# Conditioned two-stage block on one core: loads of the first half reordered, first rows stored through the scalar queue, weight sums, scales and token sums placed elsewhere

## The chip, the core and the metric

One core of a Trainium2 chip runs the whole block. The metric is device time in microseconds (us), the median of the timed runs. Engine names are those of the profile: PE multiplies matrices (PEld is its weight load), DVE is the vector engine, ACT the scalar engine, POOL the general-purpose engine, SP the engine that mostly issues DMAs. A name with a q (SPq, ACTq) is the issue of a DMA by that engine's queue. The profile's numbers come from one profiled execution.

## The reference, cut to what is computed

There are 32 sequences of 128 tokens with 512 features, one condition vector for each sequence, and a mask of tokens.

```python
emb = silu(t) @ ada_w + ada_b                      # [32, 1536]
shift, scale, gate_msa = split(emb, 3, axis=1)
norm = where(m, layernorm(x) * (1 + scale) + shift, 0)
fwd = gelu(norm @ ssm_w1 + ssm_b1, exact) @ ssm_w2 + ssm_b2
bwd = flip(gelu(flip(norm) @ bwd_w1 + bwd_b1, exact) @ bwd_w2 + bwd_b2)
x = x + gate_msa * where(m, fwd + bwd, 0)
shift_mlp, scale_mlp, gate_mlp = split(silu(t) @ ffada_w + ffada_b, 3, axis=1)
h = gelu((layernorm(x) * (1 + scale_mlp) + shift_mlp) @ ff_w1 + ff_b1, tanh)
out = x + gate_mlp * (h @ ff_w2 + ff_b2)
```

The two branches of the first half act on each token alone, so the kernel treats them as one network with 1024 hidden features, and it runs this first half only for the masked tokens. The second half runs for all 4096 tokens, in float32.

## The kernel before, in words

**First half.** The masked tokens are gathered into 512 slots: four chunks of 128 slots, two chunks (256 slots, "s0") first and two ("s1") later. The kernel first loads ada_w in `load_ada` (L124): four loads of columns 0 to 1023 (L128, shift and scale), then one load of columns 1024 to 1535 (L130, the gate). From these `modulation` makes rows of mod1 in PE (`pm_ss` for shift and scale, `pm_g` for the gate). `slot_part` (L274) spreads such rows over the slots, `modulated` (L167, L168, DVE) normalises, `transposed_slots` (L175, PE, and a copy by ACT, L176) turns the chunk, and `hidden` (L184 in PE, L188 in ACT) makes the eight parts of the hidden layer, each of four multiplications and one activation. `project` (L198) multiplies back, one multiplication for each of the eight parts, and DVE adds the bias (L200), multiplies by the gate (L201) and adds the row itself (L289). `finish_slots` stores the 128 rows into x1_rows in DRAM (L290). There are four such stores.

**Order.** From the opening on, each engine carries out its instructions in the order of the program (a manual schedule), so the order of the lines is the order of every queue. DMAs of SP and ACT share eight completion semaphores in turn: an issue waits for the DMA that used its semaphore eight issues earlier. A DMA is thus never only a transfer, it is also a place in SP's or ACT's program.

**What stands where before.** `pm_g` is multiplied in four blocks of k, strewn between the turning of the two chunks (L495 to L524); its tile of ada_w shares a buffer with the next one, ffada_w, whose load (L128 again, `ada_f`) thus waits for the last block. After the first six parts of s0 and the projections of s0 come pm_f (the second half's modulation, L254), eight parts of s1 (`ph_s`, L184) and the projections of s1, `po_s` 2 and 3.

**Second half.** The 32 sequences go in four pairs of groups of four. Both products use a scheme of seven block products (named P1 to P7) with sums of blocks: sums of weight blocks made once (`Weights.combine`, L308; `weight_sums`, L577, whose four results go through DRAM as t_rows and come back as `tw`), and sums of token blocks (`TokenBlocks.one`, L757; `token_sums`, L817 to L827). Pair 0 is prepared during the end of the first half: `take_first_half` (L656, POOL) gathers x1_rows over the rows of x for the masked tokens and so waits for the stores of L290; `Statistics` (L688, L689) and `normalised` (L700) work on DVE; side 0 is turned by DVE (L1132) and sixteen DMAs (`turned`, L727, eight by SP and eight by ACT); side 1 is turned by PE (`transposed`, L716). `scale_and_shift` then applies scale and shift of the sequence, by DVE (L708) or ACT (L710). Then `FirstProduct` begins (L888 in PE).

These are the lines around the junction:

```python
    h1 = hidden(xT_t, NH, w1, 0, AF.Gelu, "s1", ssm)
    nc.scalar.activation(warm, biasT[0:1, 0:1], AF.Gelu_apprx_tanh)
    ...
    turned(xn, xT[0], (nc.sync, nc.scalar))
    for k in range(KC // 2, KC):
        scaled(0, xT[0], k)
    ...
    finish_slots(2, h1, gs[0])
```

Of the kernel before, what the change touches and what calls it, by code (L numbers as in the profile page):

```python
# [9 lines left out]
F32 = mybir.dt.float32  # L10
# [3 lines left out]
AF = mybir.ActivationFunctionType  # L14
# [8 lines left out]
def kernel(  # L23
# [49 lines left out]
    nc = tc.nc  # L73
# [40 lines left out]
    def broadcast_rows(t, vec, queue):  # L114

        n = vec.shape[0] // D
        each = t.shape[0] // n
        for j in range(n):
            queue.dma_start(
                t[j * each : (j + 1) * each, :],  # L120
                vec[ts(j, D)].rearrange("(o d) -> o d", o=1).to_broadcast([each, D]),
            )

    def load_ada(w, which, split):  # L124

        t = adap.tile([P, KC, 3 * D], F32, tag="ada", name=f"ada_{which}")
        for k in range(KC):
            nc.sync.dma_start(t[:, k, :split], w[ts(k, P), :split])  # L128
        if split < 3 * D:
            nc.sync.dma_start(  # L130
                t[:, :, split:], w[:, split:].rearrange("(k p) d -> p k d", p=P)
            )
        return t

    modb_a = adap.tile([3 * B, D], F32, tag="modb", name="modb_a", bufs=1)
# [5 lines left out]
    w2 = ssm.tile([P, HC, D], F32, name="w2")  # L141
    ada_a = load_ada(ada_w, "a", 2 * D)


# [46 lines left out]

    def project(i, h, w, bias, gate, name, between=None):

        po = ps_o.tile([P, 512], F32, tag="o", name=f"po_{name}_{i}")
        for f in range(HC):
            if between and f in between:
                between[f]()
            nc.tensor.matmul(po, h[f][:, ts(i, P)], w[:, f, :], start=(f == 0), stop=(f == HC - 1))  # L198
        t = tp.tile([P, D], F32, tag="t", name=f"t_{name}_{i}")
        nc.vector.tensor_tensor(t, po, bias, ALU.add)  # L200
        nc.vector.tensor_tensor(t, t, gate, ALU.mult)  # L201
        return t
# [48 lines left out]
    def modulation_matmuls(pm, ada, lo, hi, blocks):  # L251
        for k in blocks:
            for j in range(lo, hi):
                nc.tensor.matmul(  # L254
                    pm[ts(j, B), :],
                    sT[:, k, :],
                    ada[:, k, ts(j, D)],
                    start=(k == 0),
                    stop=(k == KC - 1),
                )  # L260

    def modulation_rows(pm, mod, modb, lo, hi):
        rows = slice(lo * B, hi * B)
        nc.vector.tensor_tensor(mod[rows], pm[rows], modb[rows], ALU.add)
# [14 lines left out]
    def slot_part(at, j, pool, tag):  # L279
        return of_slots(pick, at, mod1, j, pool, tag, f"part{j}_s{at}")  # L280
# [6 lines left out]
    def finish_slots(at, h1, gate, between=None):  # L287
        t = project(at % (NC // 2), h1, w2, b2, gate, f"s{at}", between)
        nc.vector.tensor_tensor(t, t, xc[at], ALU.add)  # L289
        nc.sync.dma_start(x1_rows[ts(at, P), :], t)  # L290

# [31 lines left out]
    def load_x(p, spare=()):  # L323
        return [load_side(p, side, spare[2 * side : 2 * side + 2]) for side in range(2)]
# [136 lines left out]

    for j, w in enumerate((ssm_w1, bwd_w1)):
        part = w1[:, :, ts(j, D)]
        nc.gpsimd.memset(part[0:1, 0, 0:1], 0.0)
        nc.sync.dma_start(part, w.rearrange("(k p) f -> p k f", p=P))
    for j, w in enumerate((ssm_w2, bwd_w2)):
        part = w2[:, ts(j, KC), :]
        nc.gpsimd.memset(part[0:1, 0, 0:1], 0.0)
        nc.sync.dma_start(part, w.rearrange("(k p) f -> p k f", p=P))
    for key, vec in (("ssm1", ssm_b1), ("bwd1", bwd_b1), ("ff1", ff_b1)):  # L470
# [15 lines left out]
    rows = [(slot_part(c, 1, ps_o, "o"), slot_part(c, 0, ps_h, "h")) for c in range(2)]  # L486
    pm = ps_o.tile([P, 512], F32, tag="o", name="pm_g")
    xT_s = ssm.tile([P, KC, NH], F32, tag="xT", name="xT_s0", bufs=2)
# [8 lines left out]
    ]  # L497
    modulation_matmuls(pm, ada_a, 2, 3, range(2))
    fw1 = fwp.tile([P, KC, FF], F32, name="fw1")
# [9 lines left out]
    for t, vec in ((b2, ssm_b2), (b2b, bwd_b2), (modb_f, ffada_b), (fb2, ff_b2)):  # L509
        broadcast_rows(t, vec, nc.sync)  # L510
    nc.sync.dma_start(fw2, ff_w2.rearrange("(k p) f -> p k f", p=P))
    x_of = {0: load_x(0)}
    transposed_slots(xn_s[0], xT_s[:, :, ts(0, P)], "s0")
    modulation_matmuls(pm, ada_a, 2, 3, range(2, 3))
    token_i = find_slots(1)
    gather_slots(token_i)
    transposed_slots(xn_s[1], xT_s[:, :, ts(1, P)], "s1")
    modulation_matmuls(pm, ada_a, 2, 3, range(3, KC))
    ptr = ps_t.tile([P, 512], F32, tag="tr", name="ptr_b")
# [4 lines left out]
    nc.vector.tensor_copy(slot_i, ptr[:, n_bias : n_bias + B])  # L524
    modulation_rows(pm, mod1, modb_a, 2, 3)

# [31 lines left out]
    }  # L558
    t_sum[3], t_sum[4] = t_sum[1], t_sum[2]

# [27 lines left out]
    for c in range(2):  # L588
        h1 += hidden(xT_s, NH, w1, 0, AF.Gelu, "s0", ssm, range(4 * c, 4 * c + 3))
        rows = slot_part(2 + c, 1, ps_o, "o"), slot_part(2 + c, 0, ps_o, "o")  # L590
        gs.append(keep_gate(c, slot_part(c, 2, ps_o, "o")))
        xn_s.append(modulated(xc[2 + c], *rows, f"s{2 + c}", xn[:, 2 + c]))
        if c == 0:
            Weights(fw1, KC // 2, FF // 2, t_1).combine(0, 1, 2, 3)
        h1 += hidden(xT_s, NH, w1, 0, AF.Gelu, "s0", ssm, range(4 * c + 3, 4 * c + 4))
        if c == 1:
            transposed_slots(xn_s[0], xT_t[:, :, ts(0, P)], "s2")
# [5 lines left out]
    finish_slots(0, h1, gs[0])  # L603
    transposed_slots(xn_s[1], xT_t[:, :, ts(1, P)], "s3")
    nc.vector.tensor_scalar(modb_f[B : 2 * B], modb_f[B : 2 * B], 1.0, None, ALU.add)
    finish_slots(1, h1, gs[1])
# [40 lines left out]
    nc.vector.tensor_tensor(fb2_step, fb2[:, D // 2 :], fb2[:, : D // 2], ALU.subtract)  # L647
    weight_sums(3)
    weight_sums(4)
# [61 lines left out]

    def transposed(g, xn, xT, k, by_vector):

        ptr = ps_t.tile([P, 512], F32, tag="tr", name=f"ptr_{g}_{k}")
        for i in range(G):
            nc.tensor.transpose(ptr[:, ts(i, P)], xn[i][:, ts(k, P)], ident)  # L716
        for i in range(G):
            scale_and_shift(xT[:, k, ts(i, P)], ptr[:, ts(i, P)], k, g * G + i, by_vector)

# [8 lines left out]

    def scaled(g, xT, k, by_vector=False):

        for i in range(G):
            t = xT[:, k, ts(i, P)]
            scale_and_shift(t, t, k, g * G + i, by_vector)

# [380 lines left out]
    nc.gpsimd.dma_start(gate_rows, mod2[2 * B : 3 * B, :])  # L1115
    h1 = hidden(xT_t, NH, w1, 0, AF.Gelu, "s1", ssm)
    nc.scalar.activation(warm, biasT[0:1, 0:1], AF.Gelu_apprx_tanh)
    fw2_of = Weights(fw2, HC // 2, D // 2, t_2)
# [11 lines left out]
    for i in range(G):  # L1130
        t = stats[0].normalised(i, xn[:, :, i])
        nc.vector.transpose(t, t)  # L1132
    turned(xn, xT[0], (nc.sync, nc.scalar))
    for k in range(KC // 2, KC):
        scaled(0, xT[0], k)
# [4 lines left out]
    for c in range(2):  # L1140
        both = ssm.tile([P, 2, D], F32, tag="xT", name=f"xn_0_1_{c}", bufs=2)
        for i in range(2):
            xn_b.append(stats[1].normalised(2 * c + i, both[:, i]))
    finish_slots(2, h1, gs[0])

    def turn(k):
        transposed(1, xn_b, xT[1], k, by_vector=k < KC // 2)

    def turn_and_scale(k):
        turn(k)  # L1150
        scaled(0, xT[0], k, by_vector=True)

    finish_slots(
        3,
        h1,
        gs[1],
        {3: lambda: turn_and_scale(0), 5: lambda: turn_and_scale(1), 7: lambda: turn(2)},
    )
    turn(3)
    of_x[0] = TokenBlocks(0, xT)  # L1160
    for j in (1, 2, 3):
        of_x[0].one(j)
# [10 lines left out]
    now.do(1, "P2", "P5", "P6")  # L1173
    of_x[0].one(4)
    now.do(2, "P5")
    now.do(1, "P7")
    now.with_p5(2, "22")
    now.seed(2)
    now.do(1, "P3")
    now.with_p5(2, "12")  # L1180
    for n in range(4):
        now.token_sums(1, n)
    now.do(2, "P2", "P6")
# [5 lines left out]
    for p in range(NP):  # L1189
# [4 lines left out]
        def put(w, n, f, *args):  # L1194
            fills.setdefault(w, {}).setdefault(n, []).append(lambda: f(*args))
# [19 lines left out]
        if more_pairs:  # L1215
            if p == 0:
                x_of[1] = load_x(1, spare)
                put(4, 1, fw2_of.combine, 0)
                put(5, 1, fw2_of.combine, 1)
            x_next = x_of[p + 1]  # L1220
# [110 lines left out]
    with tc.If(more > 0):  # L1331
# [11 lines left out]
        with tc.For_i(0, more, 1):  # L1343
# [12 lines left out]
            for half_no, (mod, was, wbs, bias, bcol, func) in enumerate(  # L1356
# [20 lines left out]
                gate_l = of_slots(pick_l, 0, mod, 2, ps_h, "h", f"gate_l{half_no}")  # L1377
                t = project(0, h_l, wb, bias, gate_l, f"l{half_no}")
                nc.vector.tensor_tensor(xl, xl, t, ALU.add)
# [58 lines left out]
```

## Time and profile before

| what | value |
|---|---|
| median of 3 runs | 471.65 us (471.02 to 471.98) |
| the profiled execution's own time | 470.92 us |
| its span, first to last instruction | 469.2 us |
| PE busy | 452.4 us, 96% |
| DVE busy | 334.0 us, 71% |
| ACT, POOL busy | 174.9 us, 159.4 us |
| mean granted PE clock | 0.995 |
| DMA | 70.41 MB, mean 150 GB/s |

The page has a table of the span in 40 slices of 11.73 us. Beside it the trace answers by stretches of time (busy time of each engine, the granted clock, the DMA engines' share), by waits (who waited for whom, in total, how often, the longest), and by instructions in order of time: start, duration, engine, line, operation, tiles, number of such instructions, and in brackets the idle time before with what ended it. Rows that merge several instructions give the time from the first to the last end.

### The profile page before, as it was taken

The numbers are of one execution on the slowest core, as the hardware profiler recorded it, in microseconds if no ns is written. First come the engines' busy times: TensorE is split into PE (matmuls) and PEld (weight loads), VectorE is DVE, ScalarE is ACT, GpSimd is POOL, SyncE is SP. The second block draws the span as 40 slices with busy tenths as digits, with TensorE's granted clock in tenths as the row PEclk, the third lists the DMA queues.
The fourth block names the chain that finished last, engine by engine and source line by source line (L and its number), as shares of the span: only waits on it lengthen the run. The fifth ranks groups of instructions, "written<-read, shape, count | busy, mean of one in ns | idle before, by whom it ended". The sixth has DMA issues, their size and how long they took to land.

```text
span 469.2 us, 5826 instructions
## 1 busy us (share of the span) xinstructions
PE 452.4 (96%) x2000; PEld 365.3 (78%) x2000; DVE 334.0 (71%) x538; ACT 174.9 (37%) x380; POOL 159.4 (34%) x151
## 2 busy tenths in 40 slices
PE   6899999897999999999999999999999999999995
PEld 2475384475878888888888888888888888888884
DVE  4649377999778966997687498967873995434645
ACT  3131022543365074153643712545537134462000
POOL 6200063046876000189740003897100024660000
PEclk9999999999999999999999999999999999999999
DMA  8999943490413861854068528240863341213012
GB/s 278 386 408 362 394 172 53 86 345 19 121 44 134 137 90 49 312 174 163 1 194 106 106 98 288 102 161 3 217 100 88 125 168 62 96 64 117 0 76 107
DMA packets 82194, 70.41 MB, mean 150 GB/s; under 512 B 63136, under 2 KB 63664, under 8 KB 81138
## 3 DMA queue, kind: packets, MB, share of 16 engines
q1 hardware_dynamic: 67298, 57.95, 40.1%
q0 software_dynamic: 4256, 10.75, 6.8%
q10 hardware_dynamic: 10608, 1.32, 2.0%
q8 instruction: 17, 0.28, 0.2%
q14 instruction: 15, 0.12, 0.1%
HBM read 56.83 MB, written 13.17 MB: 149 GB/s over the span
## 4 chain that ended last, share of the span: by engine, by line
PE 61%; POOL 6%; ACT 6%; DVE 5%; issue 2%; POOLq 0%; DVEq 0%
PE a_o L1068 18%; PE e_o L1068 16%; PE a_m L888 14%; PE e_m L888 12%; ACT hb L850 2%; POOL hb L972 2%; ACT ha L850 1%; POOL ha L972 1%; POOL ha L939 1%; POOL rstd L694 1%; DVE xT L827 1%; PE last L1068 1%; DVE sx L817 1%; ACT a_o L1014 1%; ACT e_o L1014 1%
## 5 line engine op out<-in xcount | busy, mean ns | idle before, releaser
L939 POOL TENSOR_TENSOR ha<-p_m,ha 128x512 f32<-128x512 f32 x20 | 27.2, 1361 | 152.7 <-ACT ha L946 143.4
L1068 PE MATMUL e_o<-fw,ha 128*128 128x256 f32 x256 | 57.9, 379 | 0.0
L710 ACT ACTIVATE xT<-xT,modT 128x128 f32<-128x128 f32 x104 | 41.0, 480 | 40.2 <-DMA xT<-xn 39.7
L1068 PE MATMUL a_o<-t,hb 128*128 128x256 f32 x240 | 54.1, 379 | 0.0
L1068 PEld LDWEIGHTS e_o<-fw,ha 128*128 128x128 f32 x256 | 48.6, 190 | 6.6
L1068 PEld LDWEIGHTS a_o<-t,hb 128*128 128x128 f32 x240 | 45.6, 190 | 6.2
L656 POOL DMA_INDIRECT x<-x_rows,slot_i x32 | 36.6, 1144 | 30.2 <-DMA x_rows<-t_s 21.3
L850 ACT ACTIVATE hb<-hb,biasT 128x256 f32<-128x256 f32 x64 | 29.0, 500 | 29.9 <-POOL hb L972 19.3
L939 POOL TENSOR_TENSOR hb<-p_m,hb 128x512 f32<-128x512 f32 x20 | 29.8, 1489 | 18.2 <-DVE hb L918 17.9
L902 ACT COPY p_m<-e_m 128x512 f32<-128x512 f32 x27 | 15.8, 585 | 50.4 <-PE e_m L888 47.1
L946 ACT COPY ha<-e_m 128x512 f32<-128x512 f32 x32 | 18.5, 577 | 30.6 <-PE e_m L888 28.6
L1068 PE MATMUL e_o<-fw,s 128*128 128x256 f32 x128 | 29.2, 381 | 0.5 <-DVE s L1022 0.4
L1068 PE MATMUL a_o<-fw,ha 128*128 128x256 f32 x128 | 29.0, 380 | 0.0
L1068 PE MATMUL a_o<-t,s 128*128 128x256 f32 x128 | 28.9, 379 | 0.0
L184 PE MATMUL ph_s<-xT_s,w 128*128 128x256 f32 x128 | 28.7, 382 | 0.0
L198 PE MATMUL po_s<-w,h_s 128*128 128x512 f32 x64 | 28.5, 592 | 0.0
L1068 PEld LDWEIGHTS e_o<-fw,s 128*128 128x128 f32 x128 | 24.1, 190 | 4.9 <-DVE s L1022 1.7
L184 PEld LDWEIGHTS ph_s<-xT_s,w 128*128 128x128 f32 x128 | 24.0, 190 | 4.7 <-ACT h_s L188 1.5
L1068 PEld LDWEIGHTS a_o<-fw,ha 128*128 128x128 f32 x128 | 24.2, 190 | 3.5 <-ACT a_o L1014 0.2
L1068 PEld LDWEIGHTS a_o<-t,s 128*128 128x128 f32 x128 | 24.3, 190 | 3.3
L913 DVE TENSOR_TENSOR e_m<-a_m,ha 128x512 f32<-128x512 f32 x20 | 13.9, 696 | 17.1 <-POOL ha L939 6.6
L850 ACT ACTIVATE ha<-e_m,biasT 128x256 f32<-128x256 f32 x48 | 20.0, 467 | 14.9 <-PE e_m L888 9.6
(206 smaller groups left out, 878.1 us busy)
## 6 DMA issues: line engine op xcount, KB each, us to landing
tw<-t_rows SPq DMA_DIRECT2D x16, 896.0 KB, 5.2
x<-in_x_dram SPq DMA_DIRECT2D x16, 512.0 KB, 9.3
gate<-gate_rows POOLq DMA_DIRECT2D x8, 1024.0 KB
out_dram<-x SPq DMA_DIRECT2D x15, 512.0 KB, 3.1
xT<-xn SPq DMA_DIRECT2D x92, 64.0 KB, 2.7
fw<-in_L_cond_ff_w_dram SPq DMA_DIRECT2D x2, 2048.0 KB
ada_f<-in_L_cond_ffada_w_dram SPq DMA_DIRECT2D x4, 768.0 KB, 13.6
ada_a<-in_L_cond_ada_w_dram SPq DMA_DIRECT2D x4, 512.0 KB, 5.5
```

The lines of the kernel that those rows point to most:

```text
L184: nc.tensor.matmul(ph[:, :n], w[:, k, ts(f, P)], xT[:, k, :], start=(k == 0), stop=(k == KC - 1))
L198: nc.tensor.matmul(po, h[f][:, ts(i, P)], w[:, f, :], start=(f == 0), stop=(f == HC - 1))
L656: nc.gpsimd.indirect_dma_start(out=xs[i // G][i % G // 2][:, i % 2], out_offset=None, in_=x1_rows[:slots, :], in_offset=bass.IndirectOffse ...
L710: nc.scalar.activation(out, src, AF.Identity, bias=shift, scale=scale)
L850: nc.scalar.activation(dst[:, n], src[:, n], AF.Gelu_apprx_tanh, bias=biasT[:, f : f + 1])
L888: nc.tensor.matmul(bank[:, ts(n, QT)], self.w_block(j, product)[:, ts(n, P)], self.x_block(j, product), start=(product in ("P1", "P5") and ...
L902: nc.scalar.copy(p5, e)
L913: nc.vector.tensor_tensor(e, a, p5, add)
L939: nc.gpsimd.tensor_tensor(self.place(RESULT[j], c), self.p5[j], other, ALU.add)
L946: nc.scalar.copy(self.place(RESULT[j], c), src)
L972: nc.gpsimd.tensor_tensor(part, self.place("21", c), part, ALU.add)
L1068: nc.tensor.matmul(part, src[:, k, ts(i, P)], w[product][:, k, :], start=(last and k == 0), stop=True, skip_group_check=True,)
```

## The change

The order of loads on SP becomes: columns 0 to 1023 of ada_w, ssm_w1, (behind the first gathers) bwd_w1, ada_w's gate columns, ssm_w2, bwd_w2, ff_w1, ffada_w, biases, the rows of x, and only then ff_w2. `pm_g` is multiplied in one piece after the first three hidden parts of s0. The first two stores of x1_rows go by ACT's queue instead of SP's. `weight_sums(3)` moves up, between the two projections of s0, and gets a tile of its own; `weight_sums(4)` stays, into the tile of the first sums. Of the hidden layer of s1, the turning DMAs of ACT are issued between the seventh and the eighth part. ACT scales all of side 0, DVE all of side 1. The projection of chunk 3 is split: its multiplications, then the first token block sum, then its DVE part. The fourth token block sum follows the others, the token sums of stream 1 are spread over the first product, and two weight sums of ff_w2 each move one window earlier.

```diff
-        if split < 3 * D:
-            nc.sync.dma_start(
-                t[:, :, split:], w[:, split:].rearrange("(k p) d -> p k d", p=P)
-            )
         return t
+
+    def load_blocks(t, w, behind_gathers=True):
+        if behind_gathers:
+            nc.gpsimd.memset(t[0:1, 0, 0:1], 0.0)
+        nc.sync.dma_start(t, w.rearrange("(k p) f -> p k f", p=P))
...
     ada_a = load_ada(ada_w, "a", 2 * D)
+    load_blocks(w1[:, :, :D], ssm_w1, behind_gathers=False)
...
     def finish_slots(at, h1, gate, between=None):
-        t = project(at % (NC // 2), h1, w2, b2, gate, f"s{at}", between)
+        keep_slots(at, project(at % (NC // 2), h1, w2, f"s{at}", between), gate)
+
+    def keep_slots(at, po, gate):
+        t = gated(po, b2, gate, f"s_{at}")
         nc.vector.tensor_tensor(t, t, xc[at], ALU.add)
-        nc.sync.dma_start(x1_rows[ts(at, P), :], t)
+        queue = nc.scalar if at < NC // 2 else nc.sync
+        queue.dma_start(x1_rows[ts(at, P), :], t)
...
-    for j, w in enumerate((ssm_w1, bwd_w1)):
-        part = w1[:, :, ts(j, D)]
-        nc.gpsimd.memset(part[0:1, 0, 0:1], 0.0)
-        nc.sync.dma_start(part, w.rearrange("(k p) f -> p k f", p=P))
-    for j, w in enumerate((ssm_w2, bwd_w2)):
-        part = w2[:, ts(j, KC), :]
-        nc.gpsimd.memset(part[0:1, 0, 0:1], 0.0)
-        nc.sync.dma_start(part, w.rearrange("(k p) f -> p k f", p=P))
+    load_blocks(w1[:, :, D:], bwd_w1)
+    load_blocks(ada_a[:, :, 2 * D :], ada_w[:, 2 * D :])
+    load_blocks(w2[:, :KC], ssm_w2)
+    load_blocks(w2[:, KC:], bwd_w2)
...
-    modulation_matmuls(pm, ada_a, 2, 3, range(2))
...
+    x_of = {0: load_x(0)}
     nc.sync.dma_start(fw2, ff_w2.rearrange("(k p) f -> p k f", p=P))
-    x_of = {0: load_x(0)}
     transposed_slots(xn_s[0], xT_s[:, :, ts(0, P)], "s0")
-    modulation_matmuls(pm, ada_a, 2, 3, range(2, 3))
...
-    modulation_matmuls(pm, ada_a, 2, 3, range(3, KC))
...
-    modulation_rows(pm, mod1, modb_a, 2, 3)
...
         h1 += hidden(xT_s, NH, w1, 0, AF.Gelu, "s0", ssm, range(4 * c, 4 * c + 3))
+        if c == 0:
+            pm = ps_o.tile([P, 512], F32, tag="o", name="pm_g")
+            modulation(pm, mod1, ada_a, modb_a, 2, 3)
...
     transposed_slots(xn_s[1], xT_t[:, :, ts(1, P)], "s3")
+    t_sum[3] = [in_blocks(group_of_tiles("tw_3"))]
+    weight_sums(3)
...
-    weight_sums(3)
     weight_sums(4)
...
-    h1 = hidden(xT_t, NH, w1, 0, AF.Gelu, "s1", ssm)
-    nc.scalar.activation(warm, biasT[0:1, 0:1], AF.Gelu_apprx_tanh)
...
+    h1 = hidden(xT_t, NH, w1, 0, AF.Gelu, "s1", ssm, range(HC - 1))
     turned(xn, xT[0], (nc.sync, nc.scalar))
-    for k in range(KC // 2, KC):
+    h1 += hidden(xT_t, NH, w1, 0, AF.Gelu, "s1", ssm, range(HC - 1, HC))
+    nc.scalar.activation(warm, biasT[0:1, 0:1], AF.Gelu_apprx_tanh)
+    for k in range(KC):
         scaled(0, xT[0], k)
...
-    finish_slots(
-        3,
-        h1,
-        gs[1],
-        {3: lambda: turn_and_scale(0), 5: lambda: turn_and_scale(1), 7: lambda: turn(2)},
-    )
-    turn(3)
+    po = project(1, h1, w2, "s3", {1: turn(0), 3: turn(1), 5: turn(2), 7: turn(3)})
     of_x[0] = TokenBlocks(0, xT)
-    for j in (1, 2, 3):
+    of_x[0].one(1)
+    keep_slots(3, po, gs[1])
+    for j in (2, 3, 4):
         of_x[0].one(j)
...
-    of_x[0].one(4)
+    now.token_sums(1, 0)
     now.do(2, "P5")
     now.do(1, "P7")
     now.with_p5(2, "22")
     now.seed(2)
+    now.token_sums(1, 1)
     now.do(1, "P3")
     now.with_p5(2, "12")
-    for n in range(4):
-        now.token_sums(1, n)
+    now.token_sums(1, 2)
+    now.token_sums(1, 3)
...
-                put(4, 1, fw2_of.combine, 0)
-                put(5, 1, fw2_of.combine, 1)
+                put(3, 1, fw2_of.combine, 0)
+                put(4, 1, fw2_of.combine, 1)
```

## The prediction, made before the changed kernel had run

> **What bounds the kernel now.** I read the page first. PE is the bound, and the last 350 us give nearly nothing back; what this change touches lies in the first 140 us, slices 0 to 11.
>
> ```profile
> span 469.2 us, 5826 instructions
> PE 452.4 (96%) x2000; PEld 365.3 (78%) x2000; DVE 334.0 (71%) x538; ACT 174.9 (37%) x380; POOL 159.4 (34%) x151
> PE   6899999897999999999999999999999999999995
> DMA  8999943490413861854068528240863341213012
> ```
>
> The DMA engines are full in slices 1 to 4 (11.7 to 58.6 us), PE is full from slice 2 on with two dents. So I asked next who made PE wait, over the whole span (total us, times, longest):
>
> ```profile
> PE e_m L888 <- DVE e_m L932: 2.7, 2, 2.4
> PE e_m L888 <- ACT e_m L934: 1.3, 1, 1.3
> PE a_m L888 <- DVE hb L918: 1.1, 2, 0.8
> PE part_s L274 <- DVE mod L264: 0.8, 1, 0.8
> PE ptr_s L175 <- DVE xn_s L168: 0.6, 1, 0.6
> ```
>
> All but the last two lie between 90 and 133 us, where the first product begins: DVE is the late one there. The beginning, in order of time on PE:
>
> ```profile
> 14.74 1.90 PE L254 MATMUL pm_g<-ada_a,sT 128*32 128x512 f32 x4
> 17.19 0.65 PE L175 MATMUL ptr_s<-ident,xn_s 128*128 128x128 f32 x4 [0.55 <-DVE xn_s L168]
> 17.78 1.04 PE L254 MATMUL pm_g<-ada_a,sT 128*32 128x512 f32 x2
> 18.75 0.71 PE L216 MATMUL pl_s<-rank,pick 32*128 32x128 f32 x4
> 19.39 0.66 PE L175 MATMUL ptr_s<-ident,xn_s 128*128 128x128 f32 x4
> 19.98 1.04 PE L254 MATMUL pm_g<-ada_a,sT 128*32 128x512 f32 x2
> 21.18 1.13 PE L184 MATMUL ph_s<-xT_s,w 128*128 128x256 f32 x4
> ```
>
> The pm_g rows fill time in which PE waits for DVE's xn_s; from 21.18 on PE runs without a gap to 82 us. Last, the junction to the second half, from the views in order of time:
>
> ```profile
> 60.80 1.34 POOL L656 DMA_INDIRECT x<-x_rows,slot_i  x1 [21.34 <-DMA x_rows<-t_s]
> 72.53 0.47 ACT L188 ACTIVATE h_s<-ph_s,biasT 128x256 f32<-128x256 f32 x1 [1.25 <-PE ph_s L184]
> 77.16 6.66 ACTq L727 DMA_DIRECT2D xT<-xn  x8
> 86.94 3.19 ACT L710 ACTIVATE xT<-xT,modT 128x128 f32<-128x128 f32 x8 [12.42 <-DMA xT<-xn]
> ```
>
> The eighth activation of s1 (72.53) comes before ACT's eight DMA issues, which take 6.66 us. The change puts it behind them.
>
> **The change part by part**, against the profiled execution (470.92 us; span 469.2). The median is 0.73 us higher, and I add that at the end.
>
> *A. pm_g in one piece: +3.0.* Its four blocks go from idle or nearly idle places into the gapless stretch. A block is 1.90 - 1.04 = 0.86 us, four are 3.4. Against this, the turn of the second chunk waits only for its xn_s (DVE's L168 for it ends at 18.65) instead of running from 19.39, ACT's copy of it (0.58) ends near 19.97 instead of 20.66, and the first ph_s can start at about 20.05 instead of 21.18: -1.1. The weights for it now come right behind the first ada_w loads, 1 MB in the place of 1 MB, so the gathers behind them see the same queue. The gate's slot part now needs mod from pm_g: DVE's 0.69 (L264) hides behind the other two slot parts, but these three ran side by side (26.56 until ph_s at 27.63) and now the gate runs after the pair: one more 0.86 less the overlap, +0.7. Sum -1.1 + 3.4 + 0.7 = +3.0. Bounds: +4.1 if the bias rows or weights keep ph_s at 21.18, +2.3 if the three slot parts still overlap.
>
> *Loads: 0.* ada_f now waits for the later pm_g (28.8 instead of 21.05), but SP's wait rows show ff_w1, ahead of it in the same queue, landing only at 32; the cover is 3 us, and without it everything behind would slip by what is missing. The rows of x land before ff_w2 instead of behind it, about 5 us earlier; nothing waits for that, because the gathers over them wait for the x1_rows stores, and ff_w2 is first used beyond 115 us.
>
> *Weight sums 3: 0.* Three DVE operations, 0.64 + 0.64 + 0.95 = 2.2 us, go into a DVE gap of 4.5 us before t_s at 52.44, and leave the place in front of the statistics at 64.67.
>
> *Stores by ACT's queue.* Between 46.15 and 57.05 ACT has no instruction, so the waiting issue blocks only one copy (L176), whose reader ph_s comes at 61.4. The second t_s is ready at 54.65 + 3.0 = 57.7 instead of 54.65. Before, that store was behind two full MB on SP and landed at 60.7. By ACT's queue I have no row for a store beside a full SP queue: the fastest of the four stores took 2.0 us, the median is 3.7, a gather issued into the full queues at 20.85 landed at 28.9 (7.0 after its issue ended). I take 3.7, the nearest row: gathers from 61.7 instead of 60.80, so most of A's delay is won back here. [...]
>
> *B. The eighth activation behind ACT's DMA issues: +1.1 in all.* From the first gather to the end of gate_rows POOL needs 60.80 to 70.17, 9.4 us; rstd 1.04; from there to the last turned block DVE needs 72.14 to 77.12, 5.0. From 61.7 this gives 71.1, 72.3 and 77.3: the turning DMAs start where they did. Eight issues on ACT: 84.0. Activation: 84.5. PE reaches the eighth part of po_s 2 at 72.33 + 3.0 + 7 x 0.86 = 81.4, so it waits 3.1 us, where before it waited for nothing. What was late before goes: from the start of po_s 3 to the first a_m PE needed 79.3 to 89.93, 10.6 us, with waits for xn and xT; now DVE has had the time, and it takes 8 x 0.86 + 4 x 0.44 = 8.6. First a_m: 84.5 + 0.9 + 8.6 = 94.0 instead of 89.93, +4.1 in all, +1.1 beyond A. Behind the late activation ACT's queue holds the table load and the scales; ACT now scales 16 blocks of side 0, 16 x 0.4 = 6.4 us from 86.9 to 93.3, just before PE wants them.
>
> *C. Order of DVE after it: +0.7.* DVE's last turn ends at 94.6 (four groups of 1.36 instead of two, against two of 1.11), then one(1) 1.2, the three parts of t_s 2.2, one(2) to one(4) 3.6, and only then the seed e_m (0.7), for which P7 waits: 102.3 against 97.4. Then P7, hb and the second seed: PE goes on at 104.8, where the row of before has 99.98. That is +4.8.
>
> *D. Token sum (1,0): -0.8.* It now falls into DVE's wait for P7. From 99.2 to 116 DVE has no gap, so it shortens the stretch by 0.68 to 1.53 (the row beside a POOL sum); I take 0.8.
>
> *E. Two weight sums one window earlier: -1.0.* PE's 0.84 and 0.20 before 133 us stood behind the second sum (2.33 at 129.4), which is now done by then. The first sum, 1.23 plus, moves to 115.6, where it can hold up hb (L918) by at most 0.9, unless PE is slow there anyway.
>
> **Sum:** 3.0 + 1.1 + 0.7 - 0.8 - 1.0 = +3.0, so 473.9 against 470.92, and **474.7** on the median's scale.
>
> **The clock.** One stall already costs more than its length (stretch, busy time of PE, PEld, DVE, ACT, POOL, granted clock, DMA):
>
> ```profile
> 112.00:116.00 4.00, 1.60 (x8) 1.09 (x7) 4.00 (x4) 1.27 (x3) 2.16 (x2) 1.00 0.02 4
> 116.00:118.00 2.00, 2.00 (x6) 1.55 (x6) 1.93 (x6) 0.58 (x1) 0.00 (x0) 0.54 0.00 0
> ```
>
> After 2.4 us without work the clock was half for 3.4 us (116.1 to 119.6), a loss of 1.7. The new wait of 3.1, and the place at 15 to 20 us from which pm_g's filler is taken, can bring this: 474.7 + 1.7 = 476.4. Shorter waits in the trace (1.3, 0.8) did not. [...]
>
> **Rivals.**
> - *Forecast, 474.7 (0.42):* as summed.
> - *The chain is quicker, 472.7 (0.16):* the store lands after 2.0 as its fastest row, and the gathers run without the two t_rows stores that lay beside them at 62 to 68. The turning starts 2 us earlier and PE waits 1.1. For it: the sums now stored earlier. Against: the DMA engines are full until about 61 with a third t_rows store.
> - *Clock, 476.4, or 476.4 + 1.7 = 478.1 if both places are hit (0.22):* the half clock of the rows above, for it the length of the wait, against it the shorter waits that went unpunished.
> - *The store does not profit, 478.0 (0.08):* it lands after 7.0 like that gather, 3.3 us more of waiting; the change doesn't do what it says.
> - *Faster, 470.0 (0.12):* DVE's shorter list at the beginning of the first product decides. If the activation isn't late (B is -2.0 instead of +1.1), the 2.4 us stall at 113.3 shrinks by D and the half clock after it never comes: 3.0 - 2.0 + 0.7 - 0.8 - 1.0 - 1.7 = -1.8. It decides once PE's wait for the eighth activation is below about 1.8 us; my chain says 3.1.
>
> **Range and chances.** The two ends that I leave out are most of the faster case and the far end of clock and store: 471.5 to 478.2. A measurement of this kernel tells apart about 0.2%, 0.9 us. Faster: most of the last rival, 0.1. Same: its rest and part of the quicker chain, 0.1. Slower: 0.8.
>
> **What would show it.** A: ph_s starts near 20, pm_g is one row of 3.6 us, the fourth hidden part starts near 30.6 instead of 27.63. Stores: first gather between 60 and 62; later than 63 means the store did not profit. B: ACT's issues before the last L188 of s1, that activation near 84, and a new row, PE po_s waiting for ACT h_s, of about 3 us. C and D: the first seed near 102, no L817 right behind the second. E: no wait for hb near 133. Clock: stretches at 0.5 after 17 or 84, none at 116. It is wrong above all if the turning starts well before 76 or PE's wait for h_s is under 1 us.

## The result: slower by 2.7%, and the profile after

The changed kernel takes **483.78 us** (median, 482.26 to 485.59) beside 471.33 us (470.29 to 471.98) for the kernel before on the same chip: a ratio of 1.0268, 95% interval 1.0217 to 1.0319. The prediction was 474.7 with a range of 471.5 to 478.2. The sign was right; the size was not. The profiled executions take 482.32 and 470.92 us, so 11.4 us have to be found.

The page of the changed kernel, the same lines as were shown of before; slices are now 12.0 us:

```profile
span 480.6 us, 5829 instructions
...
PE   6699999779699999999999999999999999999996
...
PEclk9799999899999999999999999999999999999999
DMA  8979952527130864483217717530576160304013
```

All that is lost lies in the first 11 slices again. PE is weak in slices 1 (6 instead of 8), 7 and 8 (7 and 7 instead of 8 and 9) and 10 (6 instead of 9), and the row of the granted clock, which had no dent, has two. The waits of PE, over the whole span (total us, times, longest):

```profile
PE a_m L893 <- DVE hb L923: 4.2, 1, 4.2
PE po_s L200 <- ACT h_s L190: 3.5, 1, 3.5
...
PE ptr_s L177 <- DVE xn_s L170: 2.8, 1, 2.8
PE a_m L893 <- DVE t_s L206: 1.7, 1, 1.7
```

The second row was predicted (about 3). The first was not, and the third grew from 0.6. By stretches of time (stretch, busy time of PE, PEld, DVE, ACT, POOL, granted clock, DMA) each of the three long waits has half the clock behind it:

```profile
18.00:25.00 7.00, 6.69 (x21) 5.07 (x22) 2.82 (x7) 1.31 (x3) 2.37 (x3) 0.51 1.05 391
86.00:89.50 3.50, 0.90 (x2) 0.49 (x3) 1.41 (x4) 1.41 (x2) 0.00 (x0) 1.00 1.03 145
89.50:93.00 3.50, 3.50 (x9) 1.84 (x8) 2.92 (x6) 2.66 (x8) 0.00 (x0) 0.54 0.14 32
126.00:130.70 4.70, 1.13 (x5) 1.03 (x6) 4.63 (x7) 0.00 (x0) 2.86 (x2) 1.00 0.04 7
130.70:134.00 3.30, 3.30 (x10) 2.63 (x9) 1.97 (x6) 1.17 (x2) 1.13 (x2) 0.50 0.67 202
```

Ahead of the last slice, before had one such stretch, 3.4 us at 116; now there are 6.8, 3.4 and 3.4 us. The beginning on PE in order of time (start, duration, instruction, count), first before, from the first hidden part on, then after:

```profile
21.18 5.45 PE L184 MATMUL ph_s<-xT_s,w 128*128 128x256 f32 x24
26.56 1.13 PE L274 MATMUL part_s<-mod,pick 32*128 32x512 f32 x6
27.63 7.17 PE L184 MATMUL ph_s<-xT_s,w 128*128 128x256 f32 x32
```

```profile
18.02 1.10 PE L177 MATMUL ptr_s<-ident,xn_s 128*128 128x128 f32 x4 [2.79 <-DVE xn_s L170]
20.20 1.11 PE L177 MATMUL ptr_s<-ident,xn_s 128*128 128x128 f32 x4
21.99 6.87 PE L186 MATMUL ph_s<-xT_s,w 128*128 128x256 f32 x24
28.79 3.62 PE L260 MATMUL pm_g<-ada_a,sT 128*32 128x512 f32 x8
32.34 1.97 PE L280 MATMUL part_s<-mod,pick 32*128 32x512 f32 x6
34.25 1.99 PE L186 MATMUL ph_s<-xT_s,w 128*128 128x256 f32 x8
```

`pm_g` is one row of 3.62 as predicted, but the same hidden parts that took 5.45 take 6.87, and the fourth part starts at 34.25 instead of 27.63: 6.6 later, where I had 3.0. The junction, again in order of time:

```profile
65.55 1.07 POOL L661 DMA_INDIRECT x<-x_rows,slot_i  x1 [23.07 <-DMA x_rows<-t_s]
...
81.00 7.03 ACTq L732 DMA_DIRECT2D xT<-xn  x8
88.07 0.47 ACT L190 ACTIVATE h_s<-ph_s,biasT 128x256 f32<-128x256 f32 x1 [10.18 <-DMA xT<-xn]
88.60 2.67 PE L200 MATMUL po_s<-w,h_s 128*128 128x512 f32 x4 [3.48 <-ACT h_s L190]
```

The mechanism of step B is to be seen row by row: ACT issues eight DMAs for 7 us, then makes the eighth activation, then PE goes on. It all happens 4 us later than I had it, since the first gather comes at 65.55 and not at 61.7. And a place that I had as a gain, DVE and POOL in the first product, in order of time:

```profile
121.74 0.68 DVE L832 TENSOR_TENSOR xT<-xT,xn_sy 128x512 f32<-128x512 f32 x1
...
123.28 4.84 DVE L318 TENSOR_TENSOR t<-fw 128x1024 f32<-128x1024 f32 x1
123.31 1.29 POOL L944 TENSOR_TENSOR ha<-p_m,ha 128x512 f32<-128x512 f32 x1
124.54 1.27 POOL L944 TENSOR_TENSOR hb<-p_m,hb 128x512 f32<-128x512 f32 x1
125.77 1.26 POOL L973 TENSOR_TENSOR ha<-ha 128x512 f32<-128x512 f32 x1
128.86 0.66 DVE L923 TENSOR_TENSOR hb<-a_m,p_m 128x512 f32<-128x512 f32 x1
```

The moved weight sum (L318) takes 4.84 us instead of 1.2 to 1.7 (1.66 at 122.73 in before), beside three sums of POOL; hb stands behind it, and PE waits 4.2 us for hb.

### The profile page after: what moved, and what is told of

The parts are those of the page before. It is cut to its first block, busy times and chain, and to the rows that moved or that the text cites. A ratio compares the mean times of both kernels' runs of the same rounds, so it can differ in the third digit from the quotient of the medians.

```text
span 480.6 us, 5829 instructions
## 1 busy us (share of the span) xinstructions
PE 456.1 (95%) x2000; PEld 369.1 (77%) x2000; DVE 334.7 (70%) x538; ACT 175.4 (36%) x380; POOL 160.5 (33%) x151
## 4 chain that ended last, share of the span: by engine, by line
PE 72%; DVE 8%; POOL 6%; ACT 5%; issue 5%; DMA 2%; ACTq 1%; POOLq 0%; DVEq 0%
PE a_o L1073 18%; PE e_o L1073 15%; PE a_m L893 15%; PE e_m L893 12%; PE po_s L200 5%; PE ph_s L186 3%; POOL hb L977 2%; ACT hb L855 2%; POOL x L661 1%; POOL rstd L699 1%; DVE t L318 1%; ACT ha L855 1%; POOL ha L977 1%; DMA xT<-xn 1%; POOL ha L944 1%
## 5 line engine op out<-in xcount | busy, mean ns | idle before, releaser
L715 ACT ACTIVATE xT<-xT,modT 128x128 f32<-128x128 f32 x112 | 44.1, 480 | 30.5 <-DMA xT<-xn 30.0
L661 POOL DMA_INDIRECT x<-x_rows,slot_i x32 | 38.5, 1205 | 31.7 <-DMA x_rows<-t_s 23.1
L944 POOL TENSOR_TENSOR hb<-p_m,hb 128x512 f32<-128x512 f32 x20 | 28.8, 1439 | 25.0 <-issue 24.7
L200 PE MATMUL po_s<-w,h_s 128*128 128x512 f32 x64 | 30.2, 616 | 3.5 <-ACT h_s L190 3.5
L186 PE MATMUL ph_s<-xT_s,w 128*128 128x256 f32 x128 | 30.1, 395 | 0.1
L186 PEld LDWEIGHTS ph_s<-xT_s,w 128*128 128x128 f32 x128 | 25.0, 198 | 5.3 <-ACT h_s L190 0.8
L918 DVE TENSOR_TENSOR e_m<-a_m,ha 128x512 f32<-128x512 f32 x20 | 13.9, 697 | 16.3 <-POOL ha L944 6.6
```

The source lines that it names most:

```text
L186: nc.tensor.matmul(ph[:, :n], w[:, k, ts(f, P)], xT[:, k, :], start=(k == 0), stop=(k == KC - 1))
L661: nc.gpsimd.indirect_dma_start(out=xs[i // G][i % G // 2][:, i % 2], out_offset=None, in_=x1_rows[:slots, :], in_offset=bass.IndirectOffse ...
L715: nc.scalar.activation(out, src, AF.Identity, bias=shift, scale=scale)
L918: nc.vector.tensor_tensor(e, a, p5, add)
L944: nc.gpsimd.tensor_tensor(self.place(RESULT[j], c), self.p5[j], other, ALU.add)
```

## The experiments

**Theory after the result.** Three costs that have nothing to do with each other: (1) `pm_g` leaves PE idle at 15 to 20 us, which halves the clock, and takes its own time in a gapless place; (2) the eighth activation behind ACT's issues, with a half clock after the wait; (3) the weight sum that meets three POOL sums, with the same. **Rivals:** the reordered loads, the store by ACT's queue and the gathers make pair 0 late by themselves; the half clocks are accidents; POOL's sums would have held any DVE operation there.

### Undoing each of the three, and all

`u1_pieces`: pm_g's four pieces (the first is shown) and its load put back, and with it the first half of w1 behind the gathers.

```diff
-    load_blocks(w1[:, :, :D], ssm_w1, behind_gathers=False)
+    load_blocks(ada_a[:, :, 2 * D :], ada_w[:, 2 * D :], behind_gathers=False)
...
+    modulation_matmuls(pm, ada_a, 2, 3, range(2))
```

> After with pm_g back in its four early pieces, and for that the gate columns of ada_w loaded right behind its first columns and the half of w1 back behind the gathers; all else as in after (471.3 us before, 483.8 after). Theory (three separate costs: filler taken from PE, the activation behind ACT's issues, the weight sum behind POOL's sums): no half clock at 18 to 25 us, the fourth hidden part starts near 27.6 instead of 34.25, the turning DMAs near 77 instead of 81, but PE's wait for the eighth activation grows from 3.5 to about 5.4, because PE arrives earlier than the chain over the gathers; total about 479. Rival (the first half's loads and the store by ACT's queue make the chain late by themselves): the first gather stays near 65 and the total above 481. Third reading (the half clock at 18 to 25 is an accident and costs nothing by its place): the gain is at most 3.

Measured: 479.72 us (479.08 to 482.19), 1.019 of before (1.0144 to 1.0236). The fourth hidden part starts at 28.10, there is no half clock at 18, and PE now waits longer for the activation:

```profile
PE po_s L200 <- ACT h_s L190: 6.2, 1, 6.2
```

So (1) costs 4.1, and the rest of its delay was already being waited for elsewhere. But the first gather comes at 63.62, 2.8 later than in before although the first half runs nearly as in before (0.5 later). That part of the rival stays alive and is taken up below.

`u2_eighth_ahead`: all eight hidden parts before the turning DMAs.

```diff
-    h1 = hidden(xT_t, NH, w1, 0, AF.Gelu, "s1", ssm, range(HC - 1))
+    h1 = hidden(xT_t, NH, w1, 0, AF.Gelu, "s1", ssm)
     turned(xn, xT[0], (nc.sync, nc.scalar))
-    h1 += hidden(xT_t, NH, w1, 0, AF.Gelu, "s1", ssm, range(HC - 1, HC))
```

> After with all eight activations of s1 ahead of ACT's turning DMA issues, as before; all else as in after. Theory: the 3.5 us wait of PE for the eighth activation and the half clock at 89.5 to 92.9 behind it go, first a_m near 95 instead of 99.9, total about 479. Rival (ACT's sixteen scales and the landing of the turned blocks set the first a_m in any case): first a_m moves by less than 2, total above 481.5.

Measured: 479.33 us (476.88 to 480.10), 1.0154 (1.0107 to 1.0202). No wait for h_s, no half clock at 89; first a_m at 96.08 instead of 99.87, with ACT's scales as they were. The rival, that the scales set the start, is out: (2) costs 4.5.

`u3_sums_late`: the two weight sums back in their windows.

```diff
-                put(3, 1, fw2_of.combine, 0)
-                put(4, 1, fw2_of.combine, 1)
+                put(4, 1, fw2_of.combine, 0)
+                put(5, 1, fw2_of.combine, 1)
```

> After with the two weight sums of the second weight matrix one window later, where before has them; all else as in after. Theory: the first of them no longer lies beside three POOL sums (4.84 us against 1.66 before), PE's 4.2 us wait for hb and the half clock at 131 to 134 go, and the 0.84 + 0.20 of before come back; total about 479.3. Rival (the POOL sums hold whatever operation DVE has there, and the clock falls at the next stall): total within 1.5 of after, 482.3 to 483.8.

Measured: 480.85 us (480.14 to 481.23), 1.0193 (1.0157 to 1.0229): 2.9 less than after, not 4.5. DVE's rows in order of time:

```profile
129.50 1.22 DVE L318 TENSOR_TENSOR t<-fw 128x1024 f32<-128x1024 f32 x1
...
135.33 0.70 DVE L918 TENSOR_TENSOR e_m<-a_m,ha 128x512 f32<-128x512 f32 x1 [3.20 <-POOL ha L973]
```

The sum takes 1.22 again and the 4.2 us wait is gone. But POOL itself is late there (its gathers of the next pair end at 125.1), DVE waits 3.2 for POOL's ha, PE 1.86 for DVE, and the clock is halved again, at 137.5 to 140.9. So one wait was partly replaced by the next in line.

`u123_all_back`: all three.

> After with all three undone at once: pm_g in pieces, the eighth activation ahead, the sums one window later. What is left of the change is the store by ACT's queue, the third weight sum's place, the order of the token sums and the scales on ACT alone. Theory: no stretch at half clock but one, as in before, and the token sums' gain of 2 to 3 us stays: 468.5 to 470. Rival (another part of the change costs what the three do not): above 473.

Measured: 472.47 us (469.72 to 473.68), 1.0011 (0.9986 to 1.0036): the loss is gone. The three alone give 4.06 + 4.45 + 2.93 = 11.4, together 11.3. They add, and with that the theory holds as a whole. That the sums agree to 0.1 us is luck: the interval of each ratio reaches about 2 us to either side. The gain that I expected to be left (468.5 to 470) is not there on the median.

### The clock, apart from pm_g's own time

`f_filler`: after, with eight matmuls of pm_g's shape in PE's idle time at 15 to 21, whose result is not used.

```diff
+    modulation_matmuls(idle, ada_a, 0, 1, range(2))
     fw1 = fwp.tile([P, KC, FF], F32, name="fw1")
...
+    modulation_matmuls(idle, ada_a, 0, 1, range(2, 3))
     token_i = find_slots(1)
...
+    modulation_matmuls(idle, ada_a, 0, 1, range(3, KC))
```

> After with eight matmuls whose result nobody reads, of the shape of pm_g's and in the three places where before has pm_g's pieces (two blocks at 15.2, one at 18.7, one near 20.8); pm_g itself stays late, in one piece. It tells the clock from pm_g's own 3.6 us. Theory: TensorE keeps its full clock at 18 to 25, pm_g's row of 3.6 stays, the fourth hidden part starts near 31 to 31.5 instead of 34.25, and the total falls by about 2.5 to 3 against after (to about 480 to 481). Rival (the half clock at 18 to 25 has nothing to do with PE's gap): half clock still there, total no less than after.

Measured: 481.29 us (478.74 to 482.34), 1.0203 (1.0134 to 1.0272). PE in order of time:

```profile
14.83 1.90 PE L260 MATMUL pm_idle<-ada_a,sT 128*32 128x512 f32 x4
...
22.04 5.45 PE L186 MATMUL ph_s<-xT_s,w 128*128 128x256 f32 x24
27.42 3.62 PE L260 MATMUL pm_g<-ada_a,sT 128*32 128x512 f32 x8
30.97 1.97 PE L280 MATMUL part_s<-mod,pick 32*128 32x512 f32 x6
32.87 7.17 PE L186 MATMUL ph_s<-xT_s,w 128*128 128x256 f32 x32
```

More work on PE, and the fourth part comes 1.4 earlier: the hidden parts take 5.45 instead of 6.87, no row before 87 us is at half clock. So the half clock at 18 comes from the emptied place. By the median 2.5 us are gained, less sure than the row, since the two intervals overlap. I expected the fourth part at 31 to 31.5; it is 32.87, because the first part starts no earlier than in after (see step A).

### One part alone on the kernel before

`e_sums_early` moves only the two weight sums (the diff of u3 the other way round), `d_order` only DVE's order of token blocks and sums:

```diff
-    for j in (1, 2, 3):
+    for j in (1, 2, 3, 4):
         of_x[0].one(j)
...
-    of_x[0].one(4)
+    now.token_sums(1, 0)
```

> Before with one edit of the change alone: the two weight sums of the second weight matrix one window earlier. Theory (what makes the first of them long is that it meets POOL's sums at that moment, not the window by itself): in before POOL has no sum between 114.2 and 118.1, so the sum at about 115.6 takes 1.2 to 1.7, hb waits at most 0.9, the 0.84 of PE before 133 goes; total 470 to 472. Rival (the window is wrong by itself): the sum is 4 to 5 us long again, a PE wait of 3 to 4 and a further half clock, total 475 to 477.

> Before with the order of the token blocks and token sums of after alone (all four blocks ahead of the first product, the first token sum where the fourth block was, the second behind the second seed). My prediction's terms C and D: the seed in front of P7 later by 1.2, one sum in DVE's wait, so within 1 us of before, with the 2.4 us wait at 113.3 and the half clock at 116 still there or little changed. Rival (this order is what took the 2.4 wait and the half clock away in after): total 467 to 468.

Measured: 471.29 us, 1.0001 (0.9974 to 1.0029), and 471.38 us, 1.0007 (0.9975 to 1.0038). Neither does anything on its own. In the first, the weight sum takes 1.21 (at 116.28) and hb is not held: the same window that costs 2.9 in after costs nothing here. In the second, the 2.94 us token sum, PE's 2.4 us wait and the half clock are all still there (117.2 to 120.6). So after's gain at this place, 2.9 where I had 0.8, is not a result of this order. What else differs: POOL's sums. In before, DVE and POOL in order of time:

```profile
111.67 1.28 POOL L939 TENSOR_TENSOR ha<-p_m,ha 128x512 f32<-128x512 f32 x1
111.78 2.94 DVE L827 TENSOR_TENSOR xT<-xT,xn_sy 128x512 f32<-128x512 f32 x1
112.90 1.26 POOL L939 TENSOR_TENSOR hb<-p_m,hb 128x512 f32<-128x512 f32 x1
```

`p_late_gathers` tests this: before, with five small DMA issues ahead of POOL's gathers, so that POOL's sums come 3 us later.

```diff
+            if p == 0:
+                for i in range(5):
+                    spare_rows = dram.tile([B, D], F32, name=f"spare_rows_{i}")
+                    put(2, 6, nc.gpsimd.dma_start, spare_rows, mod2[2 * B : 3 * B, :])
             put(2 if p == 0 else 1, 6, take_first_half, p + 1, x_next, range(G))
```

> Before with five small DMA issues (64 KB each, to rows that nobody reads) added on POOL's queue ahead of the gathers of the next pair, so that these end about 3 us later and with them POOL's two sums behind them start near 114.7 instead of 111.7. Nothing else. Theory (the 2.94 us of DVE's token sum at 111.8 come from those two POOL sums; in after and in the kernel with all three undone these lie behind it): that row falls to 0.7, PE's wait of 2.4 and the half clock at 116 to 119.6 go, total 467 to 468.5. Rival (the later POOL sums make P2 and P4 late instead, or the wait has another cause): total 470.5 or more.

Measured: 469.66 us (469.10 to 470.49), 0.9972 (0.9948 to 0.9996), with five instructions more. In order of time:

```profile
111.79 0.68 DVE L827 TENSOR_TENSOR xT<-xT,xn_sy 128x512 f32<-128x512 f32 x1
...
114.67 1.29 POOL L939 TENSOR_TENSOR ha<-p_m,ha 128x512 f32<-128x512 f32 x1
...
125.65 1.13 PE L888 MATMUL e_m<-s,fw 128*128 128x256 f32 x4 [1.56 <-DVE e_m L913]
```

The same instruction at the same time takes 0.68. The wait of 2.4 and the half clock are gone (no stretch below full clock from 10 to 150 us), but there is a new wait of 1.56 for POOL's late sums, and the total lies between the theory's 467 to 468.5 and the rival's 470.5. Without that wait it would be about 468 (an estimate, 469.66 - 1.56).

### The same without added work, and the trap again

`s_seven`: before, with the seventh gather moved up behind the sixth, where it does the delaying itself.

```diff
-            put(2, 6, take_first_half, p + 1, x_next, range(G, G + 2))
-            put(3, 4, take_first_half, p + 1, x_next, range(G + 2, G + 3))
+            put(2, 6, take_first_half, p + 1, x_next, range(G, G + 2 + (p == 0)))
+            put(3, 4, take_first_half, p + 1, x_next, range(G + 2 + (p == 0), G + 3))
```

> Before with one gather moved: the seventh of the next pair's gathers follows the first six on POOL instead of coming in the next window, so that POOL's two sums start 1.3 us later (near 113.0 instead of 111.7) and no operation is added. Theory (DVE's 2.94 us token sum at 111.8 is held by those sums; in the run with five added DMA issues it took 0.68, but the POOL sums of the next window were then 2.6 late and PE waited 1.56 for them): the row falls to 0.7, PE's 2.4 us wait and the half clock behind it go, and since POOL has 1.2 us less to do in the next window, that new wait stays under 0.5; total 467 to 468.5, faster than both kernels. Rival (1.3 us are not enough, the sums still meet the token sums): row over 2, total as before, 470.5 to 472.

Measured: **469.27 us** (468.19 to 471.20), 0.9963 (0.9939 to 0.9987): the best median, better than both kernels, though not told apart from `p_late_gathers`. By the ratio it gains 1.7 us. The profiled execution, with a span of 466.4 us, was the fastest of the twelve. The token sum takes 0.68, POOL's sums begin at 113.42, and PE's wait at P3 is 0.29. The median is a little above the 467 to 468.5 that I wrote.

`s_seven_sums_early`: the same, with the weight sums a window earlier.

> The kernel with the seventh gather moved, and the two weight sums of the second weight matrix one window earlier too, as in the change. Theory: the first weight sum, near 113.5, now meets two or three POOL sums as in after, takes 3.5 to 5 instead of 1.2, PE waits for hb again and the clock halves; total 471 to 474. Rival (DVE's sum is held only by POOL sums that wait in a row of three): 467 to 468.5 as without it.

Measured: 472.87 us (468.21 to 474.78), 1.0012 (0.9983 to 1.0042). In order of time:

```profile
113.60 4.84 DVE L308 TENSOR_TENSOR t<-fw 128x1024 f32<-128x1024 f32 x1
113.64 1.28 POOL L939 TENSOR_TENSOR ha<-p_m,ha 128x512 f32<-128x512 f32 x1
114.86 1.28 POOL L939 TENSOR_TENSOR hb<-p_m,hb 128x512 f32<-128x512 f32 x1
116.08 1.27 POOL L968 TENSOR_TENSOR ha<-ha 128x512 f32<-128x512 f32 x1
...
119.89 2.07 PE L888 MATMUL a_m<-sx,tw 128*128 128x256 f32 x4 [4.15 <-DVE hb L918]
```

The 4.84 us, PE's wait of 4.15 us and a half clock behind it are all back, in a kernel that has nothing else of the change. The half clock lasts 6.8 us here, from 118 on, where after had 3.4 (the last section has the stretches). In `e_sums_early` the same weight sum was free. The window is not the cause; meeting POOL's sums is.

### The late store: queue or bytes

Both start from the kernel with all three undone. `t_sum3_back` puts the third weight sum and its store back behind the x1_rows stores; `t_sp_store` puts the x1_rows stores back on SP's queue.

```diff
-    t_sum[3] = [in_blocks(group_of_tiles("tw_3"))]
-    weight_sums(3)
...
+    weight_sums(3)
     weight_sums(4)
```

```diff
-        queue = nc.scalar if at < NC // 2 else nc.sync
-        queue.dma_start(x1_rows[ts(at, P), :], t)
+        nc.sync.dma_start(x1_rows[ts(at, P), :], t)
```

> The kernel with all three costs undone (first gather at 63.35), with the third weight sum and its 0.92 MB store put back where before has them, behind the x1_rows store; that store stays on ACT's queue. Theory (the store by ACT's queue lands late because the 0.92 MB are now ahead of it in the same DMA engines, 2.3 us at 0.39 MB per us): first gather near 61. Rival (ACT's queue itself is slower than SP's): still 63 or later. Total within 1.5 of the kernel that it is made from.

> The kernel with all three costs undone (first gather at 63.35), with the two stores of x1_rows put back on SP's queue; the third weight sum and its store stay ahead of the second of them. Theory (bytes ahead, not the queue): first gather between 63 and 64.5, not better than by ACT's queue. Rival (ACT's queue is the slower one): first gather near 61. Total within 1.5 of the kernel that it is made from.

| kernel | second store issued | first gather | between |
|---|---|---|---|
| all three undone | 55.56 (ACT) | 63.35 | 7.8 |
| and the third sum's store behind | 54.84 (ACT) | 60.71 | 5.9 |
| and the stores on SP | 54.77 (SP) | 64.24 | 9.5 |

The bytes ahead decided it here: 0.92 MB moved behind the store made the gather 2.6 earlier. ACT's queue is no loss. Whether it is a gain is not shown: the last row speaks for 1.7 at equal bytes, but u1_pieces, with the store on ACT and the same bytes ahead as in the first row, needs 8.5 (55.16 to 63.62), and before, with SP and the bytes behind, needs 6.1 (54.7 to 60.80), next to 5.9 by ACT in the second row. Neither kernel is faster: 474.16 us (1.0058, 1.0036 to 1.0079), outside the 1.5 that I had allowed, and 471.99 us (1.0026, 1.0002 to 1.0051). In the first, PE then waits 2.2 us for DVE's xn of side 1, and in the second 3.4; both waits bring a half clock at 82 to 87, which the 1.85 of the kernel they are made from does not. An earlier gather alone buys nothing.

## Why the prediction was wrong, step by step

- **A, +3.0; it was +6.6.** `pm_g` in one piece (3.6) and the gate's slot part on its own (1.97 instead of 1.13, so 0.8) are as I had them. The step that failed is "the first ph_s can start at about 20.05 instead of 21.18: -1.1". It started at 21.99. DVE's xn_s was 0.8 later (19.48 instead of 18.65), because the gathered rows landed later (DVE's statistics of the second chunk start at 15.26 instead of 14.47); in the profiles of these kernels the first ph_s lies anywhere from 21.2 to 22.1, a scatter that I took for a fixed number. And the two turnings ran at half clock, 1.1 instead of 0.66 each. The second one did not wait only for its xn_s, as I had it: it started at 20.20, 0.7 behind xn_s, because PE was still busy with pl_s, 1.22 at half clock instead of 0.71. The hidden parts then lost another 1.4 to the clock, which f_filler shows. 3.6 + 0.8 + 0.8 + 1.4 = 6.6.
- **Weight sum 3, 0; it was 2.6 at the first gather of the kernel with all three undone.** I counted DVE's time, which is hidden, and forgot that the step also moves a 0.92 MB store ahead of the x1_rows store. I had named it only in the quicker rival. It cost nothing at the end by itself, as t_sum3_back shows.
- **Stores by ACT's queue, gathers from 61.7; they came at 65.55.** The gather came 4.2 after the store's issue, close to the 3.7 that I took for its landing, but the issue came with all of A's delay (61.30). From issue to gather, before needed 6.1 (54.7 to 60.80), so 1.9 were won back, near the 2.1 that I had counted on (3.0 less 0.9). The gather is 4.75 later than in before because A was 6.6 and not 3.0. That the gain comes from ACT's queue is not shown.
- **B, +1.1; it was +3.3** (first a_m +9.9, less A's 6.6). The wait was 3.48 where I had 3.1. The rest is the half clock behind it, 3.4 us at half, 1.7 lost. The kernel with the activation ahead gains 4.5 in total.
- **C, +0.7:** right (the second P2 is 10.6 late, the first a_m 9.9; 0.8 in d_order alone).
- **D, -0.8:** by itself right, too: from the second P2 to the first e_m of P2 in stream 6, d_order needs 15.14 and before 15.74, so -0.6. The -2.9 seen in after is another matter: POOL's sums, moved by the late gathers, no longer met the token sum. I had not counted on that, so the rest of this gain is luck.
- **E, -1.0; it was +3.4** (7.7 late before it, 11.1 behind: 4.16 for the new wait and 1.7 for its half clock, less the 1.7 and 0.84 that before lost in the same place). The step that failed is "it can hold up hb (L918) by at most 0.9". I took POOL's places from the profile of before. But A and B move the gathers of the next pair from 103.46 to 113.84, and the sums that follow them onto exactly this weight sum. I had taken the 1.53 of "the row beside a POOL sum" as a price for D, had the 2.94 row in the same trace, and did not ask which other rows could be met.
- **The clock.** I had it as a rival at 1.7 for each place, two places, and gave it 0.22. Both named places were hit, and a third that I did not name. 476.4 to 478.1 was too low because one place lasted 6.8 us and because E changed sign. On the size of the wait that is punished, the rows of before (1.3 not, 2.4 yes) were a good guide: 2.8, 3.5 and 4.2 were all punished. The length is not what told them apart, though: a wait of 1.86 was punished and one of 1.85 was not (last section).

The upper end of the range failed because I let at most one rival happen at a time. A, B, E and the clock all went to their bad ends together, and they are not independent: a late A shifts everything that E meets.

## What to carry to other kernels

When a step is moved, its DMAs move too: here 0.92 MB of store, moved ahead, made the first gather 2.6 us later, so price what stands behind them on the queues as you price the engine's time. When a change shifts one engine by several microseconds, place the other engines' rows anew before pricing an operation beside them: the same weight sum took 1.21 us in e_sums_early and 4.84 in after, depending on what POOL did at that moment. Idle time on PE that a filler matmul covers was not free to take here: without the filler the hidden parts lost 1.4 us to the clock. In these runs each of the 16 stretches of 3.41 us with PE busy for 0.42 or less was followed by one at half clock (next section), so I would price such a gap as itself and 1.7, half of a stretch. Shorter waits need not cost more than themselves: 1.56 in p_late_gathers and 1.85 in u123_all_back did not, 1.86 in u3_sums_late and 2.2 in t_sum3_back did.

## What the runs showed of the hardware that I had not expected

- **DVE behind POOL.** DVE's sums of two operands that both lie in SBUF took 0.68 (512 elements, at 121.74 in after) or 1.22 (1024, at 129.50 in u3_sums_late) alone, 2.94 beside two POOL sums (512, at 111.78 in before), and 4.84 beside three (1024, in after and in s_seven_sums_early). The rows of hb and e_m, which read one operand from PSUM, and the statistics took 0.65 to 0.70 in before and after, beside POOL's sums as without them. The normalising row (L700), which reads one tile, took up to 1.49 beside them (at 142.87 in before), against 0.50 to 0.64 alone, so one operand was not always spared. In after, the weight sum ended at 128.12, 1.09 behind the last of three POOL sums in a row (123.31 to 127.03), and 4.84 less 1.22 is 3.6, where the three take 3.7: as if DVE had been held until they were done (an estimate from these rows). At other places, as at 129.4 in before, the row was only 2.33 and POOL's next sum took 2.26 instead of 1.26. What decides the order stays open.
- **The clock changed on a grid of 3.41 us, not by the length of a wait.** Within each of the 14 traces of this case the granted clock changed only at whole multiples of 3.41 us from one another (in after at 18.09, 24.91, 89.77, 93.18, 130.73 and 134.14), and the stretches at half clock ahead of the last slice lasted 3.41 us, 6.83 or, once, 10.24 (16.6 to 26.8 in u2_eighth_ahead). Cut along this grid, two waits of 4.16 and 4.15 us for the same hb look like this (columns as in the stretches above: PE's busy time comes first behind the stretch, the granted clock third from the end; first after, then s_seven_sums_early):

```profile
123.90:127.32 3.42, 1.51 (x8) 0.98 (x6) 3.42 (x1) 0.59 (x1) 3.26 (x4) 1.00 0.01 2
127.32:130.73 3.41, 1.16 (x5) 1.06 (x6) 3.34 (x7) 0.00 (x0) 1.70 (x1) 1.00 0.05 10
130.73:134.14 3.41, 3.41 (x9) 2.70 (x8) 1.99 (x7) 1.17 (x2) 1.27 (x2) 0.50 0.68 210
```

```profile
114.66:118.07 3.41, 1.08 (x6) 0.60 (x4) 3.41 (x1) 0.58 (x1) 2.69 (x3) 1.00 0.01 5
118.07:121.49 3.42, 1.60 (x4) 1.33 (x5) 3.32 (x9) 0.00 (x0) 0.00 (x0) 0.50 0.00 0
121.49:124.90 3.41, 3.41 (x10) 2.69 (x9) 1.54 (x4) 1.17 (x2) 1.57 (x2) 0.50 0.55 183
```

  In after the first stretch, with PE busy for 1.51 of 3.41 us (0.44), is not punished and the second (0.34) is; in the other kernel the first (0.32) is punished and the second (0.47), itself at half clock, is followed by a second half. Over the 14 traces, from the first record of the clock on (10.36 in before, 11.26 in after) and without the last 25 us of each, 16 stretches of the grid at full clock had PE busy for 0.42 or less, and each was followed by half the clock; of four between 0.44 and 0.47 two were; of all with 0.50 or more none was. So the length of a wait was only a rough guide here: waits of 1.86 (u3_sums_late, punished) and 1.85 (u123_all_back, not) both lie in stretches with PE busy for 1.56 us. Why the half clock sometimes stays for a second or third stretch although PE is busy for most of it, as at 18.1 to 24.9 in after (6.53 of 6.82 us), is not settled here.
